# Set-up of a gated cross-attention kernel: W1's outer Strassen sums by ScalarE and accumulating DMAs, and a second Strassen step in two products of mp with W2

## The chip, the cores and the metric

The kernel runs on one core of a Trainium2 chip. The metric is the device time of one execution in microseconds (us). A core has TensorE (PE, matmuls), VectorE (DVE), ScalarE (ACT), GpSimd (POOL) and SyncE (SP, which only issues DMAs here), each with its own instruction queue that is worked off in order; semaphores tie them together. Sixteen DMA engines move data for all queues.

## The reference

For each of 8 batches, with x of 1024 x 1024 and a context of 64 x 512, all in float32:

```python
memory_proj = einsum('bme,de->bmd', memory, W_mem)
scores = einsum('bnd,bmd->bnm', hidden_states, memory_proj) / sqrt(D)
attn = softmax(scores, axis=-1)
memory_context = einsum('bnm,bmd->bnd', attn, memory_proj)
gate_input = concatenate([hidden_states, memory_context], axis=-1)
gate = sigmoid(einsum('bnf,df->bnd', gate_input, W_gate) + b_gate)
fused = hidden_states + gate * memory_context
out = rmsnorm(fused, norm_w)
```

## The kernel before, in words

W_gate is split: W1 is the half that meets x, W2 the half that meets the memory context. The kernel computes mp = memory x W_mem^T (512 rows, all batches) and mg = mp x W2 once, in a set-up, so that the loop needs only x x W1 and the small product of the attention weights with mp and mg.

All large products use Strassen's algorithm in Winograd's form: a product of 2 x 2 blocks is made of seven products instead of eight, with sums of blocks on the left, sums on the right, and sums of the results. The main loop takes 16 tiles of 512 rows of x. Each goes through seven outer products (1 to 7), and each of these through seven inner ones of 128 rows and 256 columns (banks kA to kF). The right sides of the outer products are the four blocks of W1, named 1, 7, 2 and 3 (`outer_b`), and three sums of blocks: 5, 6 and 4. Block 7 is itself replaced by a sum. Each of the seven has inner sums (`inner_sum`, four per product): T1, T2 and T4 in scratch tiles it1 to it7, and R12 in place.

The set-up comes first. TensorE's order there: the products pm1, pm2, pm5, pm6, pm7, pm3 and pm4 give mp transposed (tiles mpT in four blocks, m11 to m22). Then the products of mp with W2, one level of Strassen, 1, 6, 5, 2, 7, 4 and 3 (`mg_product`, two row halves of four matmuls of 512 columns each), give mg in four blocks c11, c12, c21 and c22, which are stored to DRAM. Then the main loop starts. W2's blocks are b11, b12, b21 and b22; its right sums are t1, t2, b12 (in place) and, for product 4, b21 minus t2.

Beside this, in the set-up, DVE and GpSimd form the sums. DVE sums W1's outer blocks (`outer_sum`, 128x2048 each), adds products from PSUM, transposes mp into the scratch tiles it2, it3, it4 and it6 for storing (`store_mp`, tiles mpq), and transposes the first x tile (xq, `transpose_x`) into the tiles a11 to a22, which take over mpT's buffers. GpSimd makes W2's right sums, the inner sums of 1, 7, 5, 6 and 4, and the left sums (l) of the first outer product. SP issues, in order: the weights, four stores of mpT, four loads of xq, sixteen stores of mpq, a load of mp, the stores of c11, c22, c21 and c12, the reload of mg, and the next xq.

Every recorded operation is kept in program order on its engine (`pin`), so the order in the source is the order in each queue. A wait holds all that stands behind it on that engine. PSUM has eight banks; `setup_bank` hands them out in turn, so a product waits until the sums that read the bank's earlier content are done. A few lines carry most of this:

```python
def tt(eng, o, a, b, op):                 # L94, the operations shown under L95
    pin(eng.tensor_tensor(o, a, b, op))
setup_banks = ["b0", "b1", "b2", "b3", "b4", "ctx", "ctx", "sc"]
pgs = mg_product(4, m22, b21)             # L581
pgs = mg_product(3, s2, b22)              # L587
```

Of the kernel before, what the change touches and what calls it, by code (L numbers as in the profile page):

```python
# [8 lines left out]
F32 = mybir.dt.float32  # L9
AF = mybir.ActivationFunctionType  # L10
ALU = mybir.AluOpType
# [4 lines left out]
P = 128  # L16
# [4 lines left out]
def tile_gated_cross_attention_rmsnorm(  # L21
# [42 lines left out]
    nc = tc.nc  # L64
    B, N, D = x.shape
# [5 lines left out]
    KD = D // P  # L71
    KE = E // P
    H = 512
    C = 256
# [4 lines left out]
    const = ctx.enter_context(tc.tile_pool(name="const", bufs=1))  # L79
    gpool = ctx.enter_context(tc.tile_pool(name="gpool", bufs=7))  # L80
    xqpool = ctx.enter_context(tc.tile_pool(name="xqpool", bufs=1))
    apool = ctx.enter_context(tc.tile_pool(name="apool", bufs=1))
    rot = ctx.enter_context(tc.tile_pool(name="rot", bufs=2))
    small = ctx.enter_context(tc.tile_pool(name="small", bufs=1))
# [4 lines left out]
    pin = tc.keep_in_program_order  # L89

    def mm(o, lhsT, rhs, start, stop):
        pin(nc.tensor.matmul(o, lhsT, rhs, start=start, stop=stop, skip_group_check=True))  # L92

    def tt(eng, o, a, b, op):  # L94
        pin(eng.tensor_tensor(o, a, b, op))  # L95

    def load(o, i):
        pin(nc.sync.dma_start(o, i))

    def t4k(pool, shape, tag, name):  # L100
        return pool.tile(shape, F32, tag=tag, name=name)

    def rows_by_chunk(w, n):

        return w.rearrange("(p j) f -> p j f", j=n)

    def chunks(t, n):

        return t.rearrange("p s e -> p (s e)").rearrange("p (m j) -> p j m", j=n)
# [25 lines left out]
    w2 = []  # L135
    for k in range(KD):
        t = t4k(*((gpool, [P, D], "gate") if k < 7 else (apool, [P, D], "s4")), f"w2_{k}")
# [12 lines left out]
    def load_xq(q):  # L150
        b, n0 = q // QPB, (q % QPB) * QT
        xq[q] = t4k(xqpool, [P, 16, Q4], "xq", f"xq{q}")
        src = x[b, n0 : n0 + QT, :].rearrange("(s c) (i e) -> i c s e", c=32, i=4)
        for i in range(4):
            load(xq[q][32 * i : 32 * (i + 1), :, :], src[i])

    R11, R21, R12, R22, T4, T1, T2 = range(7)
    outer_b = {
        o: w1[h][:, :, c * H : (c + 1) * H]
        for o, h, c in ((1, 0, 0), (7, 0, 1), (2, 1, 0), (3, 1, 1))  # L160
    }
# [4 lines left out]
    def w1_place(o):  # L166

        if o in (5, 6, 4):
            outer_b[o] = const.tile([P, 4, H], F32, tag=f"t{o}", name=f"t{o}")
        inner_t[o] = const.tile([P, 3, 2, C], F32, tag=f"it{o}", name=f"it{o}")  # L170

    def w_op(o, s):
        if s >= T4:
            return inner_t[o][:, s - T4, :, :]
        k, n = {R11: (0, 0), R21: (1, 0), R12: (0, 1), R22: (1, 1)}[s]
        return outer_b[o][:, 2 * k : 2 * k + 2, n * C : (n + 1) * C]
# [34 lines left out]
    pt += [ps.tile([P, BM], F32, tag="sc", name="pt3")]  # L211


    def outer_sum(o, a, b, k=slice(0, 4)):
        tt(nc.vector, outer_b[o][:, k], outer_b[a][:, k], outer_b[b][:, k], ALU.subtract)

    def inner_sum(eng, o, n):
        s, a, b = ((T1, R12, R11), (T2, R22, T1), (R12, R22, R12), (T4, R21, T2))[n]
        tt(eng, w_op(o, s), w_op(o, a), w_op(o, b), ALU.subtract)

    def inner_sums(eng, o):
        w1_place(o)
        for n in range(4):
            inner_sum(eng, o, n)
# [3 lines left out]
    KH = KD // 2  # L228
# [6 lines left out]
    def setup_bank(name):  # L235
        nonlocal setup_next
        tag = setup_banks[setup_next % 8]
        setup_next += 1
        return (ps_ctx if tag == "ctx" else ps).tile([P, H], F32, tag=tag, name=name)
# [8 lines left out]
    def pm_product(n, l, r, k_first=False):  # L248

        pgs = [setup_bank(f"pm{n}_{i}") for i in range(2)]  # L250
        if not isinstance(l, tuple):
            l = l[:, 0], l[:, 1]
        order = [(j, k) for j in range(KH) for k in range(2)]
        if k_first:
            order.sort(key=lambda jk: jk[1])
        for j, k in order:
            o = pgs[j // 2][:, (j % 2) * HM : (j % 2 + 1) * HM]
            mm(o, l[k][:, j, :], r[:, k, :], j % 2 == 0 and k == 0, k == 1)
        return pgs

    def pm_sum(o, a, pgs):
        for i in range(2):
            js = slice(2 * i, 2 * i + 2)
            pg = pgs[i].rearrange("p (j n) -> p j n", n=HM)
            tt(nc.vector, o[:, js], a[:, js], pg, ALU.add)
# [28 lines left out]
    for k in range(2):  # L294
        pin(nc.scalar.copy(pw22[:, k], w22[:, k]))
    pgs = pm_product(2, w12, e21)
# [12 lines left out]
    pgs = pm_product(7, ps3, e12)  # L309
    pm_sum(m22, m21, pgs)  # L310
    pm_sum(m12, pu, pgs)
    w1_place(5)
    outer_sum(5, 7, 1)
    b11, b12, b21, b22 = (
        [w2[h * KH + k][:, c * H : (c + 1) * H] for k in range(KH)]
        for h in range(2)
# [2 lines left out]
    t1, t2 = ([t[:, k, :] for k in range(KH)] for t in t_w2)  # L319

    def w2_sum(eng, o, a, b):
        for k in range(KH):
            tt(eng, o[k], a[k], b[k], ALU.subtract)

    w2_sum(nc.gpsimd, t1, b12, b11)
    w2_sum(nc.gpsimd, t2, b22, t1)
    w2_sum(nc.gpsimd, b12, b22, b12)
    inner_sums(nc.gpsimd, 1)

    pgs = pm_product(3, ps4, e22)  # L330
    pm_sum(m21, m21, pgs)
# [8 lines left out]
    def transpose_x(q, t, half):  # L340

        key = q, t // 2, half
        if key not in A:
            A[key] = t4k(
                apool, [P, KH, 2 * P], f"a{t // 2 + 1}{half + 1}", f"a{t // 2 + 1}{half + 1}_{q}"
            )
        r = t % 2
        pin(
            nc.vector.transpose(  # L349
                A[key][:, :, r * P : (r + 1) * P],  # L350
                chunks(xq[q][:, 4 * t : 4 * t + 4, :], KD)[:, half * KH : (half + 1) * KH],
            )
        )
# [27 lines left out]
    def quarters(l):  # L381
        return l[:, 0:2, 0:P], l[:, 2:4, 0:P], l[:, 0:2, P:], l[:, 2:4, P:]
# [80 lines left out]
    def load_mp(b):  # L463
        mps[b] = t4k(small, [P, KD, M], "mpb", f"mpb{b}")
        load(mps[b], mpd[:, :, b * M : (b + 1) * M])
# [15 lines left out]
    def store_mpT(r, h):  # L481
        load(mpd[:, h * KH : (h + 1) * KH, r * HM : (r + 1) * HM], mpT[r][h])
# [4 lines left out]
    def mp_step(eng, tag, pool, a, b, op):  # L487
        t = t4k(pool, [P, KH, HM], tag, f"mp_{tag}")
        tt(eng, t, a, b, op)
        return t  # L490
# [20 lines left out]
    def mg_product(n, l, r):  # L511
        pgs = []
        for t in range(2):
            pg = setup_bank(f"pg{n}_{t}")
            for k in range(KH):
                mm(pg, l[:, k, t * P : (t + 1) * P], r[k], k == 0, k == KH - 1)
            pgs.append(pg)
        return pgs

    def mg_tile(pool, tag, name):  # L520
        return t4k(pool, [P, 2, H], tag, name)

    def mg_sum(o, a, pgs):
        for t in range(2):
            tt(nc.vector, o[:, t, :], a[:, t, :], pgs[t], ALU.add)

    def store_mg(o, r, h):
        load(
            mgd[1, r * HM : (r + 1) * HM, h * H : (h + 1) * H].rearrange("(t p) e -> p t e", p=P),
            o,  # L530
        )

    s1 = mp_step(nc.vector, "s1", apool, m21, m22, ALU.add)
    s2 = mp_step(nc.vector, "s2", apool, s1, m11, ALU.subtract)
    pm_sum(m12, m12, p4)
    store_mpT(0, 1)
    load_xq(0)
    outer_sum(7, 3, 7)
    w1_place(7)
    s3 = mp_step(nc.gpsimd, "junk", small, m11, m21, ALU.subtract)  # L540
    for n in range(4):
        inner_sum(nc.gpsimd, 7, n)
    c11 = mg_tile(rot, "u", "mg_c11")
    c12 = mg_tile(rot, "u", "mg_c12")
    c21 = mg_tile(rot, "l2", "mg_c21")
    c22 = mg_tile(small, "mg", "mg_c22")
    pgs = mg_product(1, m11, b11)
    for t in range(2):
        pin(nc.scalar.copy(c11[:, t, :], pgs[t]))
    for g in (2, 3, 0, 1):  # L550
        store_mp(g)
    load_mp(0)
    pgs = mg_product(6, s2, t2)
    mg_sum(c21, c11, pgs)
    tt(nc.gpsimd, s2, m12, s2, ALU.subtract)
    for t in range(4):
        transpose_x(0, t, 0)
    for part in range(2):
        inner_s(0, 1, part)
    pgs = mg_product(5, s1, t1)  # L560
    mg_sum(c12, c21, pgs)
    w1_place(6)
    outer_sum(6, 3, 5)
    for n in range(4):
        inner_sum(nc.gpsimd, 5, n)
    pgs = mg_product(2, m12, b21)
    mg_sum(c11, c11, pgs)
    store_mg(c11, 0, 0)
    w2_sum(nc.vector, b21, b21, t2)
    w1_place(4)  # L570
    outer_sum(4, 2, 6)
    for o in (6, 4):
        for n in range(4):
            inner_sum(nc.gpsimd, o, n)
    for t in range(2):
        transpose_x(0, t, 1)
    pgs = mg_product(7, s3, b12)
    mg_sum(c22, c12, pgs)
    mg_sum(c21, c21, pgs)
    store_mg(c22, 1, 1)  # L580
    pgs = mg_product(4, m22, b21)  # L581
    mg_sum(c21, c21, pgs)
    store_mg(c21, 1, 0)
    for t in (2, 3):
        transpose_x(0, t, 1)
    outer_s(0, 1)
    pgs = mg_product(3, s2, b22)  # L587
    mg_sum(c12, c12, pgs)
    store_mg(c12, 0, 1)
    outer_s(0, 2)  # L590
    load_mg(0)

# [2 lines left out]
    due, beside = {}, {}  # L595
# [338 lines left out]
```

## Time and profile before

| | us |
|---|---|
| median of 3 runs (972.02 to 972.56) | 972.33 |
| the profiled execution's own time | 972.56 |
| its span | 970.8 |

| Engine | busy us | share of the span |
|---|---|---|
| TensorE | 959.5 | 99% |
| VectorE | 818.4 | 84% |
| GpSimd | 761.1 | 78% |
| ScalarE | 328.5 | 34% |

The granted TensorE clock was 0.996 of full speed. In the profile, L12 is line 12 of the kernel; helpers such as `mm` (L92) and `tt` (L95) put many operations on one line, so the tiles tell them apart. A row names the tile written, the tile read, the shape, the count and the times; an idle time before a group names what ended it, as inferred. "x16" counts passes: each float32 matmul runs as two.

### The profile page before, as it was taken

How to read it: one execution, taken by the hardware profiler on the slowest of the kernel's cores; microseconds unless marked ns; L12 is line 12 of the kernel's file. 1: busy time of each engine (PE TensorE's matmuls, PEld its weight loads, DVE VectorE, ACT ScalarE, POOL GpSimd, SP SyncE). 2: the span in 40 equal slices, each digit the busy share in tenths (PEclk: the TensorE clock that was granted, in tenths of full speed). 3: DMA queues.
4: the chain of work that ended last, by engine and by line, in shares of the span. 5: the costliest groups of instructions: out<-in, count | busy, mean ns of one | idle time of the engine just before them, and what ended most of it. 6: DMA issues, size and time to landing. Idle time of an engine off the chain costs nothing.

```text
span 970.8 us, 14402 instructions
## 1 busy us (share of the span) xinstructions
PE 959.5 (99%) x4986; PEld 774.9 (80%) x4986; DVE 818.4 (84%) x1482; ACT 328.5 (34%) x604; POOL 761.1 (78%) x889
## 2 busy tenths in 40 slices
PE   9999999999999999999999999999999999999995
PEld 8646878788888888788888888888887878888884
DVE  6988879879797988979797978979797978979787
ACT  2000234161423334161433324152333425152345
POOL 4997878778786978878786978878687878878692
PEclk9999999999999999999999999999999999999998
DMA  9856573482919374482918375381917465391712
GB/s 378 271 141 163 98 131 98 114 169 72 178 66 166 97 144 105 108 176 66 184 65 159 102 137 113 95 188 55 195 67 146 115 129 121 87 196 48 189 69 86
DMA packets 70919, 128.32 MB, mean 132 GB/s; under 512 B 12352, under 2 KB 49216, under 8 KB 70592
## 3 DMA queue, kind: packets, MB, share of 16 engines
q1 hardware_dynamic: 61520, 93.34, 37.0%
q0 software_dynamic: 9184, 33.56, 18.9%
q8 instruction: 39, 0.64, 0.3%
q10 hardware_dynamic: 144, 0.52, 0.1%
q14 instruction: 32, 0.26, 0.1%
HBM read 87.56 MB, written 41.68 MB: 133 GB/s over the span
## 4 chain that ended last, share of the span: by engine, by line
PE 98%; DVE 1%; issue 0%; ACT 0%; DVEq 0%
PE kA L92 20%; PE pc L92 12%; PE kE L92 11%; PE kD L92 10%; PE kF L92 10%; PE kB L92 10%; PE kC L92 10%; PE psT L92 6%; PE pg L92 5%; PE pm L92 3%; PE pz L92 0%; PE pa L443 0%; PE sc L417 0%; PE pt L196 0%; DVE gate L749 0%
## 5 line engine op out<-in xcount | busy, mean ns | idle before, releaser
L95 POOL TENSOR_TENSOR gate<-gate,u 128x256 f32<-128x256 f32 x336 | 287.5, 887 | 107.5 <-DVE u L95 107.5
L662 ACT ACTIVATE gate<-gate 128x512 f32<-128x512 f32 x128 | 80.5, 631 | 306.9 <-DVE gate L95 306.1
L349 DVE STREAM_TRANSPOSE a<-xq 128x512 f32<-128x512 f32 x128 | 137.9, 1099 | 2.7 <-POOL it L95 2.7
L95 POOL TENSOR_TENSOR l<-a 128x256 f32<-128x256 f32 x128 | 122.0, 953 | 21.6 <-PE kA L92 20.4
L92 PE MATMUL pc<-mg,attnT 64*128 64x256 f32 x512 | 127.5, 389 | 0.0
L92 PE MATMUL kB<-it,l 128*128 128x256 f32 x448 | 115.1, 379 | 0.2 <-DVE gate L95 0.2
L92 PE MATMUL kD<-it,l 128*128 128x256 f32 x448 | 115.0, 379 | 0.0
L92 PEld LDWEIGHTS pc<-mg,attnT 64*128 64x128 f32 x512 | 90.6, 186 | 29.9 <-issue 21.2
L691 DVE SCALAR_TENSOR_TENSOR gate<-gate,ss,nw_sb 128x512 f32<-128x512 f32 x120 | 110.6, 931 | 1.1
L95 POOL TENSOR_TENSOR l<-s 128x256 f32<-128x256 f32 x96 | 78.0, 813 | 36.1 <-PE kF L92 35.9
L92 PE MATMUL kA<-w,a 128*128 128x256 f32 x384 | 98.6, 379 | 0.0
L92 PEld LDWEIGHTS kB<-it,l 128*128 128x128 f32 x448 | 85.0, 190 | 12.1 <-DVE gate L95 0.6
L92 PEld LDWEIGHTS kD<-it,l 128*128 128x128 f32 x448 | 85.1, 190 | 11.6
L95 DVE TENSOR_TENSOR gate<-gate,pc 128x512 f32<-128x512 f32 x128 | 86.7, 678 | 0.4 <-ACT gate L662 0.4
L95 DVE TENSOR_TENSOR gate<-gate,kE 128x256 f32<-128x256 f32 x112 | 45.5, 419 | 47.1 <-PE kE L92 41.1
L92 PEld LDWEIGHTS kA<-w,a 128*128 128x128 f32 x384 | 71.7, 190 | 9.5 <-DVE s L95 0.2
L815 ACT COPY u<-kA 128x256 f32<-128x256 f32 x112 | 40.5, 361 | 110.3 <-PE kA L92 106.0
L92 PE MATMUL kE<-it,a 128*128 128x256 f32 x256 | 69.0, 392 | 0.0
L676 ACT ACTIVATE junk<-gate 128x1024 f32<-128x1024 f32 x60 | 63.5, 1058 | 10.5 <-DMA gate<-in_x 9.5
L92 PE MATMUL kA<-t,s 128*128 128x256 f32 x256 | 65.8, 379 | 0.0
L92 PE MATMUL kC<-w,l 128*128 128x256 f32 x256 | 65.7, 379 | 0.0
L92 PE MATMUL kF<-w,l 128*128 128x256 f32 x256 | 65.7, 379 | 0.0
(140 smaller groups left out, 2041.0 us busy)
## 6 DMA issues: line engine op xcount, KB each, us to landing
xq<-in_x SPq DMA_DIRECT2D x64, 512.0 KB, 10.3
gate<-in_x POOLq DMA_DIRECT2D x60, 512.0 KB, 8.1
out<-gate SPq DMA_DIRECT2D x60, 512.0 KB, 2.6
w<-in_w_gate_t SPq DMA_DIRECT2D x8, 512.0 KB, 10.0
w<-in_w_gate_t SPq DMA_DIRECT2D x2, 2048.0 KB, 17.1
mg<-mgd SPq DMA_DIRECT2D x16, 256.0 KB, 3.8
mpd<-mpT SPq DMA_DIRECT2D x4, 512.0 KB, 7.0
mgd<-mpq SPq DMA_DIRECT2D x16, 128.0 KB, 3.6
```

The source lines that it names most:

```text
L92: pin(nc.tensor.matmul(o, lhsT, rhs, start=start, stop=stop, skip_group_check=True))
L95: pin(eng.tensor_tensor(o, a, b, op))
L349: nc.vector.transpose(A[key][:, :, r * P : (r + 1) * P], chunks(xq[q][:, 4 * t : 4 * t + 4, :], KD)[:, half * KH : (half + 1) * KH],)
L662: pin(nc.scalar.activation(g, g, AF.Sigmoid))
L676: nc.scalar.activation(junk, O[q, t], AF.Square, accum_out=ss[:, t % 2 : t % 2 + 1])
L691: nc.vector.scalar_tensor_tensor(g[:, cols], g[:, cols], rstd[:, t % 2 : t % 2 + 1], nw_sb[:, cols], ALU.mult, ALU.mult,)
L815: pin(nc.scalar.copy(p1, kb["A"]))
```

## The change

The change is confined to the set-up; the main loop's code is the same.

First, the four outer sums leave DVE. ScalarE writes the negative of one block, and a DMA issued from GpSimd then adds another block of W1 to it, read again from DRAM (the path with accumulation). Sums 5 and 7 come directly after W2's t2, sum 6 after product 5 and sum 4 after product 2. Each following sum is a negation of the one before.

Second, products 4 and 3 of mp with W2 take a second Strassen step, `mg_nested`: seven products of two matmuls with 256 columns, in six banks. Its right sums are made by GpSimd and its left sums by DVE; the left sums and product 4's right sums lie in the scratch tiles it2, it3 and it4, product 3's right sums in b21's place.

Third, work moves: the inner sums of 7, 5 and 6 go from GpSimd to DVE; those of 4 stay on GpSimd and surround product 3's last sums; s3 and it1's inner sums come earlier; product 4's right sum is made earlier, into b11's place; the load of xq moves ahead of the four stores of mpT.

```diff
-    def outer_sum(o, a, b, k=slice(0, 4)):
-        tt(nc.vector, outer_b[o][:, k], outer_b[a][:, k], outer_b[b][:, k], ALU.subtract)
+    def negate(o, i):
+        pin(nc.scalar.activation(o, i, AF.Copy, scale=-1.0))
+
+    def accumulate(o, i):
+        pin(nc.gpsimd.dma_start(o, i, accum_op=ALU.add))
+
+    def outer_sum(o, b, h, c):
+        negate(outer_b[o], outer_b[b])
+        block = rows_by_chunk(w_gate_t[:D, :], KD)[:, 4 * h : 4 * h + 4, c * H : (c + 1) * H]
+        accumulate(outer_b[o], block)
...
-    w1_place(5)
-    outer_sum(5, 7, 1)
...
     w2_sum(nc.gpsimd, t2, b22, t1)
+    w1_place(5)
+    outer_sum(5, 1, 0, 1)
+    outer_sum(7, 7, 1, 1)
     w2_sum(nc.gpsimd, b12, b22, b12)
-    inner_sums(nc.gpsimd, 1)
+    load_xq(0)
...
+    def mg_nested(eng_b, eng_a, l, r, ts, ss, ut, o, beside):
+        l11, l12, l21, l22 = quarters(l)
+        s1_, s2_, s3_, s4_ = (ss[:, i] for i in range(4))
+        t1_, t2_, t3_, t4_ = ts
+        lo, hi = slice(0, C), slice(C, H)
+        for k in range(2):
+            tt(eng_b, t1_[:, k, :], r[k][:, hi], r[k][:, lo], ALU.subtract)
+            tt(eng_b, t2_[:, k, :], r[2 + k][:, hi], t1_[:, k, :], ALU.subtract)
+        for k in range(2):
+            tt(eng_b, t3_[:, k, :], r[2 + k][:, hi], r[k][:, hi], ALU.subtract)
+            tt(eng_b, t4_[:, k, :], r[2 + k][:, lo], t2_[:, k, :], ALU.subtract)
+        yield
+        tt(eng_a, s1_, l21, l22, ALU.add)
+        tt(eng_a, s2_, s1_, l11, ALU.subtract)
+        tt(eng_a, s3_, l11, l21, ALU.subtract)
+        tt(eng_a, s4_, l12, s2_, ALU.subtract)
+        yield
...
+        kb = [setup_bank(f"pn{i}")[:, :C] for i in range(6)]
...
+        product(0, l11, r11)
+        pin(nc.scalar.copy(p1_, kb[0]))
+        product(1, s2_, t2_)
+        add(u2, p1_, kb[1])
+        other()
+        product(2, s3_, t3_)
+        add(u3, u2, kb[2])
+        for n in (3, 2):
+            tt(nc.gpsimd, dst[n], dst[n], u3, ALU.add)
+        other()
+        product(3, s1_, t1_)
+        add(u4, u2, kb[3])
+        tt(nc.gpsimd, dst[1], dst[1], u4, ALU.add)
+        product(0, l12, r21, False)
+        add(dst[0], dst[0], kb[0])
+        add(dst[3], dst[3], kb[3])
+        other()
+        product(4, l22, t4_)
+        add(dst[2], dst[2], kb[4])
+        other()
+        product(5, s4_, r22)
+        add(dst[1], dst[1], kb[5])
+        yield
+
+    s3 = mp_step(nc.gpsimd, "junk", small, m11, m21, ALU.subtract)
+    inner_sums(nc.gpsimd, 1)
...
-    load_xq(0)
-    outer_sum(7, 3, 7)
     w1_place(7)
-    s3 = mp_step(nc.gpsimd, "junk", small, m11, m21, ALU.subtract)
-    for n in range(4):
-        inner_sum(nc.gpsimd, 7, n)
...
+    t4 = b11
+    w2_sum(nc.vector, t4, b21, t2)
+    for t in range(4):
+        transpose_x(0, t, 0)
     pgs = mg_product(6, s2, t2)
...
     mg_sum(c12, c21, pgs)
     w1_place(6)
-    outer_sum(6, 3, 5)
+    outer_sum(6, 5, 1, 1)
+    in_it2, in_it3, in_it4 = (
+        const.tile([P, 3, 2, C], F32, tag=f"it{o}", name=f"mg_it{o}") for o in (2, 3, 4)
+    )
...
+    nested4 = mg_nested(nc.gpsimd, nc.vector, m22, t4,
+        [in_it2[:, 0], in_it2[:, 1], in_it2[:, 2], in_it3[:, 0]], as_s(in_it3[:, 1:]),
+        t4k(small, [P, 4, C], "junk", "mg_u4"), c21,
+        [lambda n=n: inner_sum(nc.vector, 6, n) for n in range(4)])
+    next(nested4)
+    next(nested4)
+    pgs = mg_product(2, m12, b21)
+    nested3 = mg_nested(nc.gpsimd, nc.vector, s2, b22,
+        [t[:, :H].rearrange("p (k c) -> p k c", k=2) for t in w2[KH:]], as_s(in_it4[:, :2]),
+        t4k(apool, [P, 4, C], "s1", "mg_u3"), c12,
+        [lambda t=t: transpose_x(0, t, 1) for t in (2, 3)])
+    w1_place(4)
+    outer_sum(4, 6, 1, 0)
+    next(nested3)
+    next(nested3)
     for n in range(4):
-        inner_sum(nc.gpsimd, 5, n)
-    pgs = mg_product(2, m12, b21)
+        inner_sum(nc.vector, 7, n)
     mg_sum(c11, c11, pgs)
     store_mg(c11, 0, 0)
-    w2_sum(nc.vector, b21, b21, t2)
-    w1_place(4)
-    outer_sum(4, 2, 6)
-    for o in (6, 4):
-        for n in range(4):
-            inner_sum(nc.gpsimd, o, n)
     for t in range(2):
         transpose_x(0, t, 1)
+    for n in range(4):
+        inner_sum(nc.vector, 5, n)
     pgs = mg_product(7, s3, b12)
...
-    pgs = mg_product(4, m22, b21)
-    mg_sum(c21, c21, pgs)
+    next(nested4)
     store_mg(c21, 1, 0)
-    for t in (2, 3):
-        transpose_x(0, t, 1)
+    for n in (0, 1):
+        inner_sum(nc.gpsimd, 4, n)
+    next(nested3)
+    store_mg(c12, 0, 1)
+    for n in (2, 3):
+        inner_sum(nc.gpsimd, 4, n)
     outer_s(0, 1)
-    pgs = mg_product(3, s2, b22)
-    mg_sum(c12, c12, pgs)
-    store_mg(c12, 0, 1)
     outer_s(0, 2)
     load_mg(0)
```

More of the change, by code (lines that the diff above doesn't have):

```diff
@@ L531, in store_mg, with product, other, add @@
         )
+    def mg_nested(eng_b, eng_a, l, r, ts, ss, ut, o, beside):
[15 more added lines that the diff above has]
+        yield
+        r11, r22 = ([r[2 * h + k][:, n] for k in range(2)] for h, n in ((0, lo), (1, hi)))
+        r21 = [r[2 + k][:, lo] for k in range(2)]
+        t1_, t2_, t3_, t4_ = ([t[:, k, :] for k in range(2)] for t in ts)
+        kb = [setup_bank(f"pn{i}")[:, :C] for i in range(6)]
+        p1_, u2, u3, u4 = (ut[:, i, :] for i in range(4))
+        def product(n, left_, right_, start=True):
+            for k in range(2):
+                mm(kb[n], left_[:, k, :], right_[k], start and k == 0, k == 1)
+        def other():
+            if beside:
+                beside.pop(0)()
+        dst = [o[:, t, n * C : (n + 1) * C] for t in range(2) for n in range(2)]
+        def add(to, a, b):
+            tt(nc.vector, to, a, b, ALU.add)
+        product(0, l11, r11)
[21 more added lines that the diff above has]
+        yield
@@ L555, in tile_gated_cross_attention_rmsnorm @@
     tt(nc.gpsimd, s2, m12, s2, ALU.subtract)
-    for t in range(4):
-        transpose_x(0, t, 0)
     for part in range(2):
@@ L562, in tile_gated_cross_attention_rmsnorm, with as_s @@
     w1_place(6)
-    outer_sum(6, 3, 5)
+    outer_sum(6, 5, 1, 1)
+    in_it2, in_it3, in_it4 = (
+        const.tile([P, 3, 2, C], F32, tag=f"it{o}", name=f"mg_it{o}") for o in (2, 3, 4)
+    )
+    def as_s(t):
+        return t.rearrange("p a k c -> p (a k c)").rearrange("p (i k m) -> p i k m", i=4, k=2)
+    nested4 = mg_nested(
+        nc.gpsimd,
+        nc.vector,
+        m22,
+        t4,
+        [in_it2[:, 0], in_it2[:, 1], in_it2[:, 2], in_it3[:, 0]],
+        as_s(in_it3[:, 1:]),
+        t4k(small, [P, 4, C], "junk", "mg_u4"),
+        c21,
+        [lambda n=n: inner_sum(nc.vector, 6, n) for n in range(4)],
+    )
+    next(nested4)
+    next(nested4)
+    pgs = mg_product(2, m12, b21)
+    nested3 = mg_nested(
+        nc.gpsimd,
+        nc.vector,
+        s2,
+        b22,
+        [t[:, :H].rearrange("p (k c) -> p k c", k=2) for t in w2[KH:]],
+        as_s(in_it4[:, :2]),
+        t4k(apool, [P, 4, C], "s1", "mg_u3"),
+        c12,
+        [lambda t=t: transpose_x(0, t, 1) for t in (2, 3)],
+    )
+    w1_place(4)
+    outer_sum(4, 6, 1, 0)
+    next(nested3)
+    next(nested3)
     for n in range(4):
-        inner_sum(nc.gpsimd, 5, n)
-    pgs = mg_product(2, m12, b21)
+        inner_sum(nc.vector, 7, n)
     mg_sum(c11, c11, pgs)
     store_mg(c11, 0, 0)
-    w2_sum(nc.vector, b21, b21, t2)
-    w1_place(4)
-    outer_sum(4, 2, 6)
-    for o in (6, 4):
-        for n in range(4):
-            inner_sum(nc.gpsimd, o, n)
     for t in range(2):
         transpose_x(0, t, 1)
+    for n in range(4):
+        inner_sum(nc.vector, 5, n)
     pgs = mg_product(7, s3, b12)
```

## The prediction

> **What bounds the kernel now.** I read the page's totals and chain first, then TensorE's waits, then the instructions of the set-up in order of time, then the DMA traffic of the same stretch.
>
> ```profile
> span 970.8 us, 14402 instructions
> PE 959.5 (99%) x4986; PEld 774.9 (80%) x4986; DVE 818.4 (84%) x1482; ACT 328.5 (34%) x604; POOL 761.1 (78%) x889
> ...
> PE 98%; DVE 1%; issue 0%; ACT 0%; DVEq 0%
> ```
>
> TensorE carries the chain; nothing else is 2% of it. The waits of TensorE over the whole span are two:
>
> ```profile
> PE pz L92 <- DVE zeros L118: 1.2, 1, 1.2
> PE kB L92 <- DVE gate L95: 0.2, 1, 0.2
> ```
>
> So there is no hidden slack: TensorE work removed is time won, and every new TensorE wait is time lost. The products that the change replaces, in TensorE's order of time (start, us):
>
> ```profile
> 67.61 7.03 PE L92 MATMUL pg<-w,mpT 128*128 128x512 f32 x16
> 74.48 7.03 PE L92 MATMUL pg<-w,mp_s 128*128 128x512 f32 x16
> 81.35 1.03 PE L92 MATMUL kA<-w,a 128*128 128x256 f32 x4
> 82.21 1.03 PE L92 MATMUL kB<-it,l 128*128 128x256 f32 x4
> ```
>
> Starts are 6.87 apart for 16 passes (429 ns each); passes of 256 columns come at 0.86/4 = 216 ns. Product 4 starts at 67.6, product 3 at 74.5, the main loop at 81.35. Next, VectorE (DVE) and GpSimd (POOL) in the same set-up:
>
> ```profile
> 42.37 1.27 POOL L95 TENSOR_TENSOR it<-w 128x512 f32<-128x512 f32 x1
> 43.72 1.27 POOL L95 TENSOR_TENSOR it<-w,it 128x512 f32<-128x512 f32 x1
> ...
> 57.92 2.88 POOL L95 TENSOR_TENSOR l<-l,a 128x256 f32<-128x256 f32 x1
> ```
>
> ```profile
> 52.74 4.10 DVE L349 STREAM_TRANSPOSE a<-xq 128x512 f32<-128x512 f32 x4 [2.74 <-POOL it L95]
> ...
> 57.92 2.29 DVE L95 TENSOR_TENSOR t<-w,t 128x2048 f32<-128x2048 f32 x1
> ```
>
> DVE ran out of work once, for 2.74 us. The releaser named had long been done; the fourth xq load was issued at 40.6 and the slowest took 12.0 to land, so it was that load, at 52.6. Both engines otherwise work without a break to about 82, so the set-up is full on three engines, and TensorE only just isn't waiting. Last, the DMA traffic (columns: busy by engine, clock, DMA share, GB/s):
>
> ```profile
> 40.00:50.00 10.00, 10.00 (x24) 4.37 (x23) 10.00 (x11) 0.58 (x1) 9.92 (x7) 1.00 1.02 202
> 50.00:56.00 6.00, 6.00 (x15) 2.66 (x14) 3.26 (x5) 0.00 (x0) 5.92 (x5) 1.00 1.06 294
> 131.00:133.00 2.00, 2.00 (x10) 1.54 (x9) 2.00 (x4) 0.00 (x0) 0.00 (x0) 1.00 1.09 207
> ```
>
> Saturated engines move 202 GB/s while xq loads run, 294 while the transposed mp is stored, and 207 in a stretch with only accumulating loads (the residuals of L666).
>
> **What the Trainium skill says.** "SBUF — State Buffer", section Who interferes with whom: a VectorE tensor_tensor with both inputs in SBUF and a GpSimd operation exclude each other for a whole instruction; one with a PSUM input doesn't take part. The trace agrees: beside the 2.29 us DVE sum at 57.92, the GpSimd operation that takes 0.72 alone took 2.88. "DMA: Bandwidth & Descriptors", section Issuing engines are not separate DMA queues: transfers of all queues interleave on the same 16 engines. The shares near 1 above agree. "TensorE: Matmul & The Clock Gate", section What's actually happening: after an idle window of some 3.4 us TensorE runs at half clock until it has been busy as long. The kernel before has no such gap, so no run here shows it.
>
> **The change, part by part.**
>
> TensorE: 32 passes of 512 columns (13.74 us from 67.61 to 81.35) become 2 x 7 products x 2 x 2 = 56 passes of 256, 56 x 0.216 = 12.10. Gain 1.64. The nested products would run at 67.61 and 73.66, the main loop start at 79.71.
>
> Outer sums: four leave DVE (2.63, 3.38, 2.29, 3.24 = 11.5 us). Each becomes a ScalarE negation of 128x2048, by the rows of 512 (631 ns) and 1024 (1058) some 1.9 us, and an accumulating load of 1.05 MB. ScalarE is otherwise idle from 40 to 82, so its work is covered. GpSimd pays 0.88 per issue (the 60 of L666) and must wait for each negation.
>
> DVE gains the inner sums of 7, 5 and 6 (12 of 128x512, at 0.68 alone), eight quarter sums of the nested lefts and 14 PSUM sums of 256 columns (0.42 each) for four dropped ones of 512. GpSimd drops those 12, gains 16 sums of 128x256 (0.72) and six more. A quarter sum from SBUF has no row on DVE: at least the PSUM form's 0.42, at most the 1.55 that a 128x512 sum took beside GpSimd; I take 0.5, since GpSimd's operations of that stretch are short.
>
> Order on GpSimd: two issues (0.9 each) go in front of the b12 sums, and s3 in front of it1. What waits for these is product 7 (60.75 on TensorE) for b12 and s3 and the main loop for it1; GpSimd is there by about 48, so they are hidden. W2's fourth right sum moves ahead of the xq transposes on DVE (four, 1.55 each beside GpSimd) and costs nothing while DVE waits for xq anyway. The last stores of mg, its reload (3.7) and the bias load (7.2) move with TensorE: the bias landed at 101.3 and was used at 108.1, a cover of 6.8 that shifts along.
>
> Loads: load_xq moves on SP's queue ahead of the four mpT stores. It waits for the last DVE read of W_mem (22.9), so its four DMAs precede all mpT and mpq stores. The first transposes of xq overwrite mpT's buffers, so they also wait for those stores. Count the traffic from 33.5, where the weights are in (the norm weight's DMA: 14.63 + 18.9). xq: 2.1 MB at 202 = 10.4. The accumulating loads of 5 and 7, issued about 33: 2.1 MB at 207 = 10.1. The mpT stores: 2.1 MB at between 294 and the weights' 416, say 6. The first twelve mpq stores: 1.57 MB at 294 = 5.3. Sum 31.9, so the twelfth lands about 33.5 + 31.9 + 2 = 67.4; before, the sixteenth was issued by 56.9 and took some 3.6.
>
> That landing matters because the nested left sums are written into the scratch (it3, it4) that the mpq stores read. Before, its next writers came at 62 to 84, covered by the scratch's idle time; now DVE stops at the first it4 sum, and all its later work queues behind: three more quarter sums (with it 2.0), it7 (2.7), c11 (1.25), two transposes (2.1), it5 (2.7), c22 (1.25), the first c21 sum (0.63). That is 12.6, ending at 80.0. Product 3's first bank waits for this c21 sum, 6.4 after 73.66. Its third product then waits until DVE has done c21, u2, it6, u3, it6, u4, c21 (3.3 against 1.7 of TensorE): 1.6.
>
> Two waits don't depend on the DMAs. GpSimd has two it4 sums ahead of its c12 sums, and the first must wait for product 3's last matmul, which reads that scratch. From that matmul: 0.08 + 1.35 + 1.23 + 0.73 on GpSimd, 0.42 on DVE, 0.1 of hand-over = 3.9 until bank kB is free, of which kA covers 0.86: 3.1. Then kF waits for u2, which stands on DVE behind two c12 sums and two sums of 1024 (1.2 alone, 2.2 beside GpSimd): 0.5 to 1.6, I take 1.0.
>
> Sum: -1.64 + 6.4 + 1.6 + 3.1 + 1.0 = +10.5. The profiled execution took 972.56 (span 970.8, 1.8 around it), the median is 972.33: the difference of 0.2 is below what counts here. Span about 981.3, time about 982.8. I forecast **982.5**, a shade lower, as the mpT stores may go at the loads' rate.
>
> Unknowns: the mixed DMA rate was seen only for xq with residuals. If the mix flows 1.25 times faster, the landing is 61 and the 6.4 vanishes; if pieces of 2 KB accumulate a quarter slower, it comes 3 later, since they share the engines. Accumulated sum 6 is issued after the l sums, which wait for xq: about 62, landing 8 (two of half its size took 8.3 together) to 14 later. ScalarE's negation of it stands ahead of the copy that product 4's fifth step waits for (71.0), and GpSimd's issue of sum 4 ahead of nested 3's right sums. Up to about 72 this hides behind DVE's delay; at 76 it takes its place. A gap over 3.4 would cost up to 1.7 more by the clock rule. A gain from any of this is excluded: TensorE waited 0.2.
>
> **Rivals.**
> (a) Forecast, DVE late behind the stores: 978.5 to 987. For: the DMA share near 1. Against: FIFO and sharing among queues are inferred.
> (b) The DMAs are in time, and the two in-order waits and some of the 1.6 remain: -1.64 + 3.1 + 1.0 + (0 to 1.6) = +2.5 to +4, so 974.8 to 978.5 with a delay of a us or two.
> (c) Accumulating loads become the bound: sums 6 and 4 are serial, each landing late; a 14 us landing for 6 and the negation (1.9) hold product 4, then GpSimd's eight sums (5.8) hold product 3: 987 to 994.
> (d) Not slower: the shared port goes to DVE first after kB, the DMAs are in time: -1.64 + 3.1 + 0.4 = +1.9, 974.2; it decides where the gaps sum to under 3.58. Against it, GpSimd's next sum is ready before DVE's.
>
> **How the numbers follow.** (a) 0.55, (b) 0.22, (c) 0.15, (d) 0.05, else 0.03. From 974.8 (leaving (d), the lowest of (b) and the rest) to 990 (leaving (c)'s upper half) about 0.85 is held; within (a) alone 978.5 to 987. A measurement here can't tell 0.2% (1.9 us) from no change. Slower by more: 0.91; within: 0.06; faster: 0.03, since the gain of 1.64 alone is less than the bound.
>
> **What would show it.** TensorE's waits list: a wait on a DVE sum at product 3's start near 74 of several us (a), of 3 us at kB after product 3 (all cases), one at kF. DVE idle from about 58 before the it4 scratch sums, ended by mpq landings. TensorE's 56 passes 12.1 us net of gaps, or the gain is wrong. Wrong if the mpq stores land by 61, or if the kB wait is missing.

## The result and the profile after

| | before | after |
|---|---|---|
| median, us | 972.19 | 986.47 |
| runs, us | 972.02 to 972.56 (4) | 983.08 to 988.20 (4) |
| profiled execution / its span, us | 972.56 / 970.8 | 987.62 / 985.8 |
| ratio of the times | 1 | 1.0141, 95% interval 1.0129 to 1.0153 |

The changed kernel is 1.4% slower: 14.3 us in the medians, 15.0 in the two profiled spans, which all that follows is summed against. Its four runs lie within 5.1 us of each other, those of the kernel before within 0.5, and the profiled one is among its slower ones. The page's totals and its chain:

```profile
span 985.8 us, 14527 instructions
PE 962.7 (98%) x5010; PEld 781.9 (79%) x5010; DVE 820.5 (83%) x1508; ACT 337.2 (34%) x610; POOL 760.5 (77%) x903
...
PE 96%; DVE 2%; DMA 1%; POOL 0%; ACT 0%; issue 0%; SPq 0%; DVEq 0%
```

TensorE does less work and is busy 3.2 us longer, which already says that some of its passes were slow. DVE's share of the chain has grown from 1% to 2%, and DMA is new on it with 1%. TensorE's waits (us in total, times, longest):

```profile
PE pn L92 <- DVE mg_c L95: 6.5, 1, 6.5
PE kB L92 <- DVE mg_c L95: 3.0, 1, 3.0
PE pn L92 <- ACT mg_u L584: 2.2, 1, 2.2
```

Three new waits, 11.7 us, all between 71 and 96. TensorE's instructions there, in order of time (start, busy us; in brackets the idle time before and what ended it):

```profile
67.74 1.03 PE L92 MATMUL pn<-w,mpT 128*128 128x256 f32 x4
...
73.57 1.13 PE L92 MATMUL pn<-w,mpT 128*128 128x256 f32 x4 [2.21 <-ACT mg_u L584]
...
82.89 2.08 PE L92 MATMUL pn<-w,mp_s 128*128 128x256 f32 x4 [6.46 <-DVE mg_c L95]
84.76 4.72 PE L92 MATMUL pn<-w,mg_it 128*128 128x256 f32 x12
...
95.94 2.07 PE L92 MATMUL kB<-it,l 128*128 128x256 f32 x4 [3.01 <-DVE mg_c L95]
...
102.79 3.67 PE L92 MATMUL psT<-a,mpb 128*64 128x256 f32 x32
```

psT, the first matmul after the main loop's first seven inner products, starts at 102.79; before it was 87.48:

```profile
87.48 3.67 PE L92 MATMUL psT<-a,mpb 128*64 128x256 f32 x32
```

The shift of 15.3 adds up from the starts (to 15.2; the rest is a slightly slow fifth step of product 4):

| where | us |
|---|---|
| product 4 starts later (67.74 for 67.61) | +0.13 |
| passes of products 4 and 3 at full clock, 56 x 0.216 for 13.74 | -1.64 |
| start to start before product 4's fifth step (71.19 to 73.57) | +2.38 |
| start to start before product 3 (76.26 to 82.89) | +6.63 |
| product 3's 28 passes: 9.01 (82.89 to 91.90) for 6.05 | +2.96 |
| before kB (92.76 to 95.94) | +3.18 |
| kB to psT: 6.85 for 5.27 | +1.58 |

Two terms, 4.5 us, are no waits. The first four passes of product 3 take 2.08 where 1.03 is usual: the clock was halved. The granted clock changes at 78.48, 88.72, 95.55 and 98.96, all on one grid of 3.41 us. Five windows cut along this grid (columns: busy by engine, PE first, then granted clock, DMA share, GB/s):

```profile
71.65:75.07 3.42, 1.50 (x7) 1.35 (x8) 3.39 (x6) 1.86 (x2) 1.52 (x2) 1.00 0.18 41
75.07:78.48 3.41, 1.35 (x7) 0.85 (x5) 3.38 (x4) 0.00 (x0) 3.25 (x5) 1.00 0.91 158
...
81.89:85.31 3.42, 2.42 (x6) 1.98 (x7) 3.42 (x8) 0.31 (x1) 0.95 (x2) 0.50 0.66 198
...
92.13:95.55 3.42, 0.80 (x4) 0.37 (x2) 0.09 (x1) 0.37 (x1) 3.33 (x4) 1.00 0.00 0
95.55:98.96 3.41, 3.02 (x7) 2.48 (x8) 2.89 (x4) 0.00 (x0) 3.41 (x4) 0.50 0.24 89
```

Half clock begins inside the long gap and lasts 10.2 us, three of these windows; the second stretch, after kB's gap, lasts one, 3.4.

What DVE did meanwhile:

```profile
55.23 4.32 DVE L360 STREAM_TRANSPOSE a<-xq 128x512 f32<-128x512 f32 x4 [6.88 <-DMA mpd<-mpT]
...
69.49 0.42 DVE L95 TENSOR_TENSOR mg_it<-mp_s 128x256 f32<-128x256 f32 x1 [4.30 <-DMA mgd<-mpq]
...
80.96 2.47 DVE L95 TENSOR_TENSOR mg_c<-mg_c,pg 128x512 f32<-128x512 f32 x4
...
95.46 0.42 DVE L95 TENSOR_TENSOR mg_c<-mg_c,pn 128x256 f32<-128x256 f32 x1 [3.57 <-POOL mg_c L95]
```

It stopped twice for stores: 6.88 us ahead of x's transposes, which overwrite mpT's buffers, and 4.30 ahead of the left sums in it4. The row at 80.96 is four sums; its third is the c21 sum that product 3's first bank waits for, over at 82.85. ScalarE and GpSimd:

```profile
71.34 1.91 ACT L217 ACTIVATE t<-t 128x2048 f32<-128x2048 f32 x1 [15.18 <-DMA t<-in_w_gate_t]
```

```profile
92.14 1.26 POOL L95 TENSOR_TENSOR it<-t 128x512 f32<-128x512 f32 x1 [4.44 <-PE pn L92]
...
94.71 2.09 POOL L95 TENSOR_TENSOR mg_c<-mg_c,mg_u 128x256 f32<-128x256 f32 x3
```

The accumulated sum 6 lands at 71.3, and the negation that reads it stands ahead of the copy for product 4's fifth step. GpSimd's two it4 sums wait for product 3's last matmul and hold the c12 sums that kB needs. Last, the DMA traffic of the stretches that were shown of before:

```profile
40.00:50.00 10.00, 10.00 (x25) 4.40 (x24) 8.35 (x7) 0.59 (x1) 9.92 (x6) 1.00 1.11 231
50.00:56.00 6.00, 6.00 (x15) 2.66 (x14) 0.77 (x1) 1.75 (x1) 0.55 (x1) 1.00 1.09 303
```

The engines are saturated and DVE is idle for most of 50 to 56. A load of 1 MB that accumulates took 11.0 us from issue to landing (median of three; 21.0 for the fourth), the mpT stores 18.0 where they had taken 7.0.

### The profile page after: what moved, and what is told of

Same layout as the page of the kernel before. It is cut to its first block, busy times and chain, and to the rows that moved or that the text cites. A ratio compares the mean times of both kernels' runs of the same rounds, so it can differ in the third digit from the quotient of the medians.

```text
span 985.8 us, 14527 instructions
## 1 busy us (share of the span) xinstructions
PE 962.7 (98%) x5010; PEld 781.9 (79%) x5010; DVE 820.5 (83%) x1508; ACT 337.2 (34%) x610; POOL 760.5 (77%) x903
## 4 chain that ended last, share of the span: by engine, by line
PE 96%; DVE 2%; DMA 1%; POOL 0%; ACT 0%; issue 0%; SPq 0%; DVEq 0%
PE kA L92 20%; PE pc L92 12%; PE kE L92 11%; PE kD L92 10%; PE kB L92 10%; PE kF L92 10%; PE kC L92 10%; PE psT L92 6%; PE pm L92 3%; PE pg L92 3%; PE pn L92 1%; DMA mgd<-mpq 1%; DMA memq<-in_mem 1%; DVE it L95 1%; DVE mg_c L95 0%; PE sc L428 0%
## 5 line engine op out<-in xcount | busy, mean ns | idle before, releaser
L92 PEld LDWEIGHTS kA<-w,a 128*128 128x128 f32 x384 | 71.7, 190 | 9.1
```

## The experiments

The theory: the accumulating loads put DVE late, and the order of sums on DVE and GpSimd turns that into waits. Rivals: the second step alone costs the time; the loads cost it wherever they stand; the slow clock costs it. All ratios are against the kernel before.

### Each half of the change alone

The second step with the outer sums left to DVE (`e7_nested_only`), and the outer sums by loads with the products left whole (`e8_sums_only`):

```diff
# e7, on the changed kernel
-    def outer_sum(o, b, h, c):
-        negate(outer_b[o], outer_b[b])
...
+    def outer_sum(o, a, b, k=slice(0, 4)):
+        tt(nc.vector, outer_b[o][:, k], outer_b[a][:, k], outer_b[b][:, k], ALU.subtract)
# e8, on the kernel before
     w2_sum(nc.gpsimd, t2, b22, t1)
+    w1_place(5)
+    outer_sum(5, 1, 0, 1)
+    outer_sum(7, 7, 1, 1)
...
-    outer_sum(6, 3, 5)
+    outer_sum(6, 5, 1, 1)
...
-    outer_sum(4, 2, 6)
+    outer_sum(4, 6, 1, 0)
```

> The second Strassen step of products 4 and 3 alone: the four outer sums are DVE's subtractions again (11.5 us together), the rest is the changed kernel's. Theory: without the loads DVE is already full from 17 to 82 (2.5 us idle), so the 11.5 make it 9 to 10 later at product 3, which waits 7 to 9 there, with the slow clock after it; kB's 3.0 stays: 984 to 989, no better than the whole change. Rival, the loads alone make the loss and DVE has room: 976 to 979, as without loads.

> The outer sums by negation and accumulating load alone, on the kernel before; the products stay as they were and GpSimd keeps its inner sums. Theory: the loads of sums 5 and 7 put off x's landing by about 10 us (52.6 to some 62), DVE's transposes of x with it, and the W2 sum behind them comes 3 to 6 too late for product 4 at 67.6, although DVE has 11.5 us less to do: 974 to 979. Rival, the relief of DVE covers the delay and nothing on TensorE waits: 971 to 973.

Measured: 988.80, ratio 1.017 [1.0155, 1.0186], and 979.76, 1.0078 [1.0063, 1.0093]. The first theory holds; the second time lies a little above its range, and less of it comes from where it was expected. In e7, DVE is without a pause from 41 to past 89, and TensorE waits 5.7 in product 4 and 3.1 ahead of product 3:

```profile
78.06 2.08 PE L92 MATMUL pn<-mg_it,mpT 128*128 128x256 f32 x4 [5.69 <-DVE mg_c L95]
```

With the loads alone, DVE idles 11.68 us until x's transposes at 59.46:

```profile
59.46 4.08 DVE L358 STREAM_TRANSPOSE a<-xq 128x512 f32<-128x512 f32 x4 [11.68 <-DMA mgd<-mpq]
```

Product 4 then waits 1.6 for W2's sum in three pieces, and one wait that was not foreseen is larger: GpSimd's inner sums of 4 wait until 88.55 for their load, the left sums of the next product stand behind them, and kB waits 3.2 at 98. So both lose, for different reasons: e7 gives DVE too much work, e8 makes its input late and holds GpSimd for a load. e7 keeps the inner sums that the change moved to DVE as well, so the second step with nothing else was not tried.

### The loads

`e2_no_loads` leaves out all four accumulating loads, `e5_no_57` those of sums 5 and 7, `e6_no_64` those of 6 and 4; `e9_late_loads` keeps all and issues 5 and 7 later:

```diff
# e2: in outer_sum
-        accumulate(outer_b[o], block)
# e9
     w1_place(5)
-    outer_sum(5, 1, 0, 1)
-    outer_sum(7, 7, 1, 1)
+    negate(outer_b[5], outer_b[1])
+    negate(outer_b[7], outer_b[7])
...
     inner_sums(nc.gpsimd, 1)
+    outer_load(5, 0, 1)       # the accumulating load alone
+    outer_load(7, 1, 1)
```

> Leaves out the four accumulating loads, so W1's outer sums 5, 7, 6 and 4 are only negated blocks; every other operation stays. DMA theory: without their 4.2 MB the mpq stores land some 10 us earlier, DVE doesn't stop before the it4 scratch, the waits of 2.2 and 6.5 and the slow clock go, and what is left is -1.6 of TensorE plus 3.0 at kB plus up to 1.0 at kF and 1 of DVE lateness: 974.5 to 977. Rival, that DVE has too much work in the set-up whatever the DMAs do (22 more operations): a wait of several us before product 3 stays, and the time is 980 or more.

> Outer sums 5 and 7 lack their accumulating load (they are left as the negated block); sums 6 and 4 are whole. Theory: these two loads of 1 MB each stand ahead of the x loads and the stores of mp, and so DVE comes late by some 7 to 9 us to all that follows. Without them product 3's first wait (6.5) falls to nothing or to the 1.2 at its third product that the kernel without loads shows; sum 6 is issued and lands some 8 earlier, so the 2.2 at product 4 goes too; the 3.0 at kB and 1 to 2 of slow clock stay: 977 to 979.5. Rival, the late loads 6 and 4 are the bound: product 4 still waits 2 or more and the time is 981 or more.

> Outer sums 6 and 4 lack their accumulating load (they are left as the negated block); sums 5 and 7 are whole. Theory: the 2.2 at product 4 goes, since ScalarE's negation waits for no load, but DVE is as late as before for product 3, whose first wait grows by about what product 4 no longer waits, less 1 to 2 since the last stores of mp share the engines with one load less: 983.5 to 986.5. Rival, the late loads are the bound: 981 or less.

> Only the issue of the two loads of outer sums 5 and 7 is moved on GpSimd's queue, from ahead of the b12 sums (31 to 33) to behind the first inner sums (about 46); their negations stay, and nothing is left out. Theory: it is the place of these loads, ahead of x and the stores of mp, that makes DVE late; issued at 46 they leave the x landing as without them (transposes near 48 to 50 in place of 55.2), and only the mpq stores behind them come late. Product 3's first wait falls from 6.5 to between 2.4 (what is left without these loads at all) and 5; the 3.0 at kB stays: 979 to 983. Rival, 4 MB more on saturated engines cost the same wherever they stand: 985 or more.

| | median | ratio | x's transposes | product 3 starts | half clock, us |
|---|---|---|---|---|---|
| after | 986.47 | 1.0141 | 55.23 | 82.89 | 10.2 + 3.4 |
| e2, no loads | 977.97 | 1.0060 [1.0045, 1.0075] | 47.70 | 73.58 | 3.4 |
| e5, no 5 and 7 | 979.03 | 1.0068 [1.0053, 1.0083] | 50.10 | 76.17 | 3.4 |
| e6, no 6 and 4 | 985.05 | 1.0126 [1.0110, 1.0143] | 55.37 | 80.49 | 6.8 + 6.8 |
| e9, late loads | 985.24 | 1.0127 [1.0110, 1.0144] | 51.72 | 80.67 | 6.8 + 6.8 |

The first pair of loads decides: without it product 3 starts 6.7 earlier, without the second pair 2.4. TensorE without the first pair:

```profile
76.17 1.70 PE L92 MATMUL pn<-w,mp_s 128*128 128x256 f32 x4 [2.36 <-DVE mg_c L95]
...
88.12 1.13 PE L92 MATMUL kB<-it,l 128*128 128x256 f32 x4 [3.02 <-DVE mg_c L95]
```

Product 3's wait is 2.36 in place of 6.46, and kB's is untouched: it doesn't depend on the loads. DVE has no idle time before its transposes here, nor before the it4 sums: both of its stops are gone. The times of e5 and e6 end in their theories' ranges, the waits less well: e5 keeps 2.36 where at most 1.2 was expected, and in e6 product 4 still waits 1.2, for DVE, while product 3's wait falls to 4.90 where it was to grow. Without any load (e2, 1.0 above its range, below the rival's) 5.9 us of loss remain in the medians (977.97 - 972.03, the kernel before in the same measurement): 1.2 at product 3's third product, 3.1 at kB and the half clock after it.

e9 fell outside its theory's range, onto the lower edge of the rival's. The move does what was said for x (51.72), but the mpq stores then come late (DVE stops 2.1 at 60.3), sum 6 lands at 71.7 and product 4 waits 2.9. Product 3 starts 2.2 earlier; then the half clock takes 9.06 for product 3 and 8.39 from kB to psT, 6.1 us against 4.5 in the changed kernel. The gain went there, and where the half clock falls is chance in each execution (see the clock below): e9's runs are 983.37, 983.89, 986.59 and the profiled 986.77. That 4 MB cost the same wherever they stand isn't shown by this: the starts did move.

### The waits one by one

`e3_own_scratch` puts product 3's left sums into tiles of their own, so that DVE doesn't wait for the mpq stores; `e1_pool_order` moves GpSimd's two it4 sums behind product 3; `e4_fill` fills TensorE's gap ahead of product 3 with matmuls that nobody reads.

```diff
# e3
-        as_s(in_it4[:, :2]),
+        own,                      # four tiles with the tags sT, e and attnT
# e1
-    for n in (0, 1):
-        inner_sum(nc.gpsimd, 4, n)
     next(nested3)
     store_mg(c12, 0, 1)
-    for n in (2, 3):
+    for n in range(4):
         inner_sum(nc.gpsimd, 4, n)
# e4, after product 4's last matmul
+        if o is c21:
+            for _ in range(28):
+                mm(full[5][:, C : C + P], ident, ident, True, True)
```

> The left sums of nested product 3 go into small tiles that are free until the first softmax, instead of the it4 scratch that the mpq stores read; the loads stay. If it is the wait for these stores that makes DVE late, DVE goes on at 65.2 instead of 69.5, the wait before product 3 falls from 6.5 to about 2.5, the slow passes of product 3 go, and the wait at kB too, since GpSimd's it4 sum no longer waits for product 3: 976 to 979. The wait of 2.2 in product 4 stays, since it is the landing of accumulated sum 6. Rival, DVE is late by its work alone: the wait before product 3 stays above 5 and only kB's goes, 982 or more.

> The two it4 sums of GpSimd are moved behind its three c12 sums of product 3. If the wait at kB (3.0 in the changed kernel) is the queue order on GpSimd, it goes to under 0.5, the slow passes after it (some 1.6) go with it, and up to 1.0 may come back as a wait at kF: 982 to 983.5 beside 986.5. The waits before product 3 stay at 2.2 and 6.5. If kB waits for something else (the landing of accumulated sum 4, or DVE itself being late), the wait stays near 3 and the time at 986.

> 28 small matmuls into an unused half bank (6 us) stand between the nested products 4 and 3, so that TensorE is busy in most of the gap; nothing else changes. If the slow passes of product 3 come from the clock after an idle gap, its 28 passes of 256 columns run at 216 ns again (9.0 falls to 6.1), while the third product then waits about 1.6 for DVE: 983.5 to 985.5 beside 986.5, granted clock near 1 at 80 to 90. If they come from something else (operands, banks), the passes stay slow and the time the same.

Measured: e3 982.42, 1.011 [1.0095, 1.0125]; e1 984.70, 1.013 [1.0113, 1.0147]; e4 986.59, 1.015 [1.0135, 1.0165].

e3 ends in its rival's range, but product 3's wait, 3.63, lies between what theory and rival said; it is shorter also because product 4 ended later, partly at half clock, so the starts are compared here. DVE no longer stops for the mpq stores, and its left sums start at 65.74 in place of 69.49:

```profile
65.74 0.94 DVE L95 TENSOR_TENSOR mg_own<-mp_s 128x256 f32<-128x256 f32 x1
...
69.20 0.68 DVE L95 TENSOR_TENSOR it<-w 128x512 f32<-128x512 f32 x1
```

But they now run beside GpSimd's sums at 0.83 to 0.94 each, where the late ones ran alone at 0.42; of the inner sums of 5 behind them, the first takes 1.65 for 0.93. Of the 4.30, DVE keeps 1.76 at the inner sums of 7 (69.20 for 70.96), and product 3 starts 1.06 earlier (81.83). x's transposes came 0.64 later in this profile (55.87), so the wait may be worth some 1.7. psT comes 5.1 earlier in all: 2.5 of it is at kB, whose gap falls from 3.0 to 0.5, since the it4 sums no longer wait for product 3, and 1.2 in product 3's passes, where half clock lasted 3.4 us.

e1 shows that gap by itself: 0.5 in place of 3.0, and psT 4.35 earlier (98.44). Of this, 2.5 is the gap and 0.75 the way from kB to psT, where the half clock goes and kF waits 0.5; 1.1 is in product 3's passes, with 6.8 us of half clock for 10.2, and isn't the edit's. The span gains only 2.9, as a later kC and a later kB now wait 0.4 and 0.6, and the median 1.8, which is 1.2 short of what was expected.

e4 keeps the clock full to the end of the set-up. Its waits of TensorE:

```profile
PE kB L92 <- DVE mg_c L95: 3.0, 1, 3.0
PE pn L92 <- ACT mg_u L585: 1.8, 1, 1.8
PE pn L92 <- DVE mg_c L95: 1.5, 2, 1.2
...
PE kF L92 <- DVE u L95: 1.2, 1, 1.2
```

The expected gain didn't come: psT is 1.6 earlier in the profile (101.23), the median no better than the changed kernel's. Where TensorE is fast, it waits instead: 1.2 at product 3's third product and 1.2 at kF. The half clock had been covering these waits, so of its 4.5 us some 2.4 would have been lost without it too.

### Order instead of less work

`e10_spread` keeps the whole change and moves its sums: load 5 at 46, loads 6 and 7 behind product 4's right sums, load 4 behind product 3; the inner sums of 7, 5 and 4 into the main loop on DVE, those of 6 on DVE behind products 4 and 3, two each. `e11_slots` changes the loop slots of these sums; `e12_slots_dve` is e11 with the outer sums on DVE.

```diff
# e10, without the moves of the loads and of the sums of 6 and 4
-    for n in range(4):
-        inner_sum(nc.vector, 7, n)
...
-    for n in range(4):
-        inner_sum(nc.vector, 5, n)
...
-        at((3, 4, 5, 6, 22, 23, 24, 25)[i], inner_sum, nc.vector, o, n)
+    for i, o in enumerate((7, 5, 4, 2, 3)):
+        for n in range(4):
+            at(7 * i + 3 + n, inner_sum, nc.vector, o, n)
# e11, in place of the last three lines
+    for o, t in ((7, 3), (5, 15), (4, 22), (2, 29), (3, 33)):
+        for n in range(4):
+            at(t + n, inner_sum, nc.vector, o, n)
```

> Nothing is left out. The loads of 5 at 46 and of 6 and 7 behind product 4's right sums, that of 4 behind product 3; DVE's inner sums of 7 and 5 and GpSimd's of 4 go into the main loop's slots on DVE (3 to 6, 10 to 13, 17 to 20; those of 2 and 3 move to 24 to 27 and 31 to 34), and the inner sums of 6 stand behind product 4. Theory: what the change loses is order, not work: with DVE's 8 sums (some 5.5 us) out of the way of product 3 and GpSimd's two out of the way of kB, product 3 starts without a wait, kB waits 0.5 or less, kF about 1: -1.64 + 0.5 + 1.0 and a few tenths, 971 to 974.5, about the time of the kernel before. Rival, DVE is short of time everywhere: the sums moved into the loop, where DVE is busy 15.6 of the first 20 us, make TensorE wait there instead: 976 or more.

> As the spread version, and nothing left out; only the slots of the moved inner sums differ: those of 5 leave slots 10 to 13, where DVE's sum of 128x512 was held for 3.74 us beside a chain of GpSimd operations and TensorE waited 2.2 with the slow clock after it, for 15 to 18; 4 at 22 to 25, 2 at 29 to 32, 3 at 33 to 36. Theory: with this last wait gone the TensorE work saved shows at the end: psT of the first tile already starts 1.9 earlier than before, so about 970.5 to 972, equal to the kernel before or up to 0.2% faster. Rival, the loop has no room for eight to twelve sums more in any slots and gives back 2 or more elsewhere: 974 or more.

> The same slots, but the four outer sums by DVE's subtractions instead of negations and accumulating loads. Theory: DVE has 11.5 us more to do in the set-up and only some 7 us (inner sums of 7 and 5) less; product 4 or 3 waits 3 to 4 for its sums, and the slow clock follows: 974 to 977, so the loads are needed for the gain. Rival, order alone decides and the loads are worth nothing: within 1 of the version with loads.

Measured: e10 976.04, 1.0046 [1.0030, 1.0062]; e11 974.42, 1.0022 [1.0014, 1.0031]; e12 981.92, 1.0100 [1.0087, 1.0114].

In e11's set-up TensorE waits for nothing:

```profile
67.94 1.03 PE L92 MATMUL pn<-w,mpT 128*128 128x256 f32 x4
...
73.98 1.03 PE L92 MATMUL pn<-w,mp_s 128*128 128x256 f32 x4
...
80.03 1.03 PE L92 MATMUL kA<-w,a 128*128 128x256 f32 x4
```

From 67.94 to 80.03 the two products take 12.09, where they took 13.74: the saving of 1.64 is real. It is then given back: psT is 1.32 earlier than before (though product 4 starts 0.33 later), kB of the fifth outer product is level with before (113.07 for 113.09), and from 131 on TensorE is 2.15 late. In that stretch DVE is full, in the windows of the kernel before and then of e11:

```profile
104.00:131.00 27.00, 26.82 (x143) 21.84 (x142) 23.60 (x44) 6.21 (x11) 21.47 (x29) 1.00 0.49 78
```

```profile
104.00:131.00 27.00, 25.84 (x129) 20.09 (x128) 26.68 (x48) 4.25 (x7) 22.51 (x27) 1.00 0.48 69
```

26.68 of 27 us against 23.60, and the waits of TensorE that are listed there are all for DVE (0.6 at kB, 0.5 at kD). In e10 a single sum did it, held beside a chain of GpSimd operations:

```profile
94.38 3.74 DVE L95 TENSOR_TENSOR it<-t,it 128x512 f32<-128x512 f32 x1
```

It takes 0.68 alone; kB then waited 2.24 and half clock followed. Both times end in their rivals' ranges. The set-up reaches its full gain by order alone, with nothing left out, as the theories said; the loop has too little room on DVE for what was moved there, as the rivals said. As loads and sums were moved together, their shares aren't told apart. Neither version beats the kernel before. e12 is 7.5 above e11: with this order too, the outer sums on DVE cost more than the loads, and 5 more than was expected at most: psT starts 6.1 later than in e11 (92.27), after waits of 1.1 in product 4, 2.4 ahead of product 3 and 0.2 to 0.9 at four further places.

## Why the prediction was right, and where not

The sign and the range (974.8 to 990.0) held; the time was 4.0 above the forecast, in the upper part of case (a).

**TensorE's work, -1.64: right.** It was hidden in the result, and e11 shows it as 12.09 us for the 56 passes.

**Product 3 held by DVE, 6.4: the wait came, its size was off, and its cause was put at one stop of two.** The wait in the list, 6.5, agrees by chance; product 4's 2.4 belongs to the same lateness, so the term measured 9.0. The step "the twelfth lands about 67.4" was 2.1 early, and "that is 12.6" of DVE work was 13.4. More important, the prediction named the mpq stores and expected DVE idle from about 58; it was idle for 6.88 us ahead of 55.2 and for 4.30 ahead of 69.5. Taking the later wait away (e3) brings product 3 forward by 1.06 only. Taking both away (e5) brings 6.7, so most seems to lie with the earlier stop, x's transposes behind the mpT stores, which the prediction mentioned without costing it. That is a difference of two runs: no run takes away the earlier stop alone. The cost of a stop is what the engine can't make up behind it: here DVE had no slack, but the sums behind the stop ran alone at 0.42, and without the stop they share time with GpSimd's. The Trainium skill, "SBUF — State Buffer", section Who interferes with whom, says that a VectorE instruction with two SBUF inputs contends with a GpSimd instruction that reads SBUF, which the prediction used for other sums; the 0.42 alone and 0.83 to 0.95 beside GpSimd agree with it.

**Product 3's third product, 1.6, and kF, 1.0: right in mechanism, not visible.** e4 shows 1.2 and 1.2. In the changed kernel half clock stood in their place.

**kB, 3.1: right**, 3.18, by the very chain that was worked out; e1 removes it.

**Sum 6: as said.** It landed at 71.3, inside the stated 62 plus 8 to 14. Product 4 waited 2.2, and as product 3 waited for DVE anyway, which had no idle time from 69.49 to 82.85, that wait cost nothing of its own. But the loads 6 and 4 weren't cheap: without them (e6) the mpq stores take 2.8 us in place of 5.7, DVE doesn't stop for them, and product 3 starts 2.4 earlier. That queues share the engines, which the prediction called inferred, shows in the mpT stores of SP's queue too: 18.0 us, and 11.2 without loads 5 and 7 from GpSimd's (e5).

**The clock, "up to 1.7 more": too low.** It cost 2.96 and 1.58, in part in place of the two waits above. The prediction priced one window of 3.4 us. The page of the Trainium skill that it took this from, "TensorE: Matmul & The Clock Gate", says in the same section, What's actually happening, that the window is free-running. The traces agree: in each of the fourteen, all changes of the granted clock lie on one grid of 3.41 us, which begins at another place in each execution. That a gap needs 3.4 us doesn't agree: 2.24 (e10), 2.36 (e5) and 3.0 (kB) were enough.

What decides can be read from the traces, cut along their grids. Of the windows at full clock, 29 were without matmuls for 2.06 us or more, and half clock followed each; 3873 were for 2.00 or less, and it followed none. Of the windows at half clock, the 15 with 2.87 us or more of matmuls were followed by full clock, the 29 with 2.74 or less were not (ends of matmuls are modelled, so these bounds are good to about 0.1). The five windows of the changed kernel that were shown are examples: 1.50 busy kept the clock and 1.35 lost it. So the place of a gap on the grid counts beside its length: of the same 3.0 us at kB, 2.62 fell into one window in the changed kernel, and half clock followed; they fell apart into 1.90 and 1.12 in e4 and e7 and 1.72 and 1.29 in e5, and none did. As the grid's place is chance, so is a part of each single profile's difference: the 10.2, 6.8 and 3.4 us of half clock in the runs above aren't effects of their edits alone.

Summed: 9.0 for 6.4, 2.96 for 1.6, 3.18 for 3.1, 1.58 for 1.0 and the 0.13 give 4.7 more than forecast in the span (15.2 for 10.5).

Rival (b), the DMAs in time, is what e2 shows: 977.97, inside its 974.8 to 978.5; in the changed kernel they were not in time, so neither (b) nor (d), which needed the same, came about. Rival (c) named loads 6 and 4; 5 and 7 cost more (2.4 against 6.7 at product 3's start).

## What to carry to other kernels

Work that leaves a full engine for the DMA engines is only free if these have room at that time: here 2 MB of accumulating loads (5 and 7) stood ahead of stores whose buffers the relieved engine needed next. When a wait is found, ask for the one before it on the same engine, and take the lateness away to see what it was worth; the last stop isn't the cause by being last. And where TensorE is the bound, a gap of 2 to 3 us can cost as much again in clock (0 to 3.1 us after the 3.0 at kB), or hide the next wait, so waits can't be summed one by one from the list; of two gaps of one length, one may cost and the other not, by where the clock's windows fall.

## What was not expected of the hardware

- Half clock came in stretches of 3.4, 6.8 or 10.2 us, on a grid of 3.41 us, after each window with 2.06 us or more without matmuls and after none with 2.00 or less; so it came after gaps from 2.24 us on, and not after each gap of 3.0.
- Accumulating loads of 1 MB took 8.5 to 16.2 us from issue to landing, and 15.0 to 22.0 where they were issued directly behind another. Traffic in which they take part moved 231 GB/s from 40 to 50, where x's loads alone with other stores moved 202.
- A DVE sum of two SBUF inputs, 0.68 alone, was held for 3.74 us beside GpSimd operations in close succession (e10).
